# Perceiver kernel: small vectors loaded second, and the second batch's normalisation with statistics instructions and five norms on GpSimd

## The chip, the cores and the metric

The kernel runs on one core of one Trainium2 chip. The core has five engines that this text names as the profile does: PE (TensorE, matmuls, with PEld for its weight loads), DVE (VectorE), ACT (ScalarE), POOL (GpSimd) and SP (SyncE, which here only issues transfers). Each engine takes its instructions in the order in which they stand in its own queue and waits where an instruction needs something that isn't there yet. The metric is the device time of one execution in microseconds, smaller being better.

## What is computed

The input is a set of latents `x` (16 batches of 64 vectors of 128 numbers), a context of 16 batches of 1601 vectors of 128 numbers, and a mask over the context. Two layers follow each other. Each has a cross attention from the latents to the context together with the latents, and then a recurrent scan and a feed-forward part on the latents. The part that matters here is the cross attention of the first layer:

```python
xn = _layernorm(x, ln1_w, ln1_b)            # x: the context, 1601 rows a batch
ln = _layernorm(latents, ln2_w, ln2_b)
q = ln @ Wq                                  # 16 heads of 64
kv = jnp.concatenate([xn, ln], axis=-2) @ Wkv
k, v = jnp.split(kv, 2, axis=-1)
logits = jnp.einsum('bhld,bhsd->bhls', q * scale, k * scale)
out = jnp.einsum('bhls,bhsd->bhld', softmax(logits), v)
return out.reshape(B, L, INNER) @ Wo
```

`_layernorm` subtracts the mean of each row, multiplies by the reciprocal square root of variance plus 1e-5, and applies a weight and a bias.

## The kernel before

**Folding.** The kernel never forms keys and values. It multiplies the query weights with the key weights once (`fold_qk`, in four groups of four heads, L320; the result is the tile `wqk`), so that a score is a product of a folded query (`q`, L429, kept as `qT`) with the normalised context itself. In the same way `fold_vo` (tile `wvo`) merges value and output weights, and the weighted mean (`av`, L669) is taken over the normalised context.

**The context of a batch.** 1600 of its 1601 rows are held as 13 tiles of 128 columns (the last with 64 rows, filled up with the 64 latents of the batch); the remaining row is treated apart. Two forms are needed: `kv`, rows on partitions, and `kvT`, its transpose. Batch 0 is prepared by `first_context` (L467), which takes mean and variance of each tile with a pair of VectorE statistics instructions (L483, L484), raises variance plus EPS to the power −½ on POOL (L487), and has the norms of the 13 tiles done by DVE (tiles 0 to 3), ACT (4 to 7, L519) and POOL (8 to 12, L492). Every other batch of layer 0 goes through `context` (L549): two reductions on DVE give the means (L558), 13 squares with accumulated sums on ACT give the variances (L564), DVE scales them (L568), POOL computes the power (L117, inside the helper `rsqrt`) and the offset (L570), and ACT applies 13 norms (L573). Then the tiles are written to DRAM for layer 1 (`xh`, L576), transposed by PE in groups of four (`kt`, L581), copied to `kvT` by ACT (L582), and multiplied by the norm's weight, in `kvT` on ACT (L590) and in `kv` on POOL (L543, in `with_latents`).

**The main loop.** A group is half the heads of one batch; there are 64 groups, each with 13 steps. In step `n` of `run`, `scores` makes one 128 x 512 block of scores on PE (`s`, L607, in one of three PSUM buffers), ACT copies it out (`st`, L614), and DVE keeps the running maximum (`R`, L621). After the 13 steps the maximum is turned and spread over partitions (`tm`, `mb`), DVE subtracts it from two blocks at a time (L656), ACT takes the exponential (L657), and PE multiplies the result with `kv` (`av`, L669), `LAG` = 21 steps after the scores.

**Order of the work.** The preparation functions are generators. `run` resumes each of them as the steps go by: a list `prep` holds for each the step from which it is resumed, and a `yield` of a number ends its portion for this step, while a `yield` of a tuple (`HOP` and its kin) makes it pause for that many steps. Between the portions, `behind` and `in_order` fix on each engine which instruction may stand behind which. At the very beginning `setup` issues the first transfers and resumes the first generators by an explicit list (L226). The transfers of the start go through two queues: on ACT the first pair of query and key weights (`raw_pair`, L305) and then the 12 small vectors as rows (`vrow`, L202); on SP the first latents `X` (L199), the context of batch 0 in four pieces (`rkv`, L455 and L458) with the other weight pairs between and behind them, the row apart (`xe`), the vectors spread over partitions (`vec`), batch 1 (`kv`, L460) and more latents. PE transposes `vrow` to columns (`vcol`, L221), ACT copies them out (L223) and DVE makes the negative (`nvcol`, L224).

Of the kernel before, what the change touches and what calls it, by code (L numbers as in the profile page):

```python
# [32 lines left out]
F32 = mybir.dt.float32  # L33
# [3 lines left out]
AF = mybir.ActivationFunctionType  # L37
ALU = mybir.AluOpType
# [4 lines left out]
P = 128  # L43
NB, L, D = 16, 64, 128
# [20 lines left out]
HOP1, HOP, HOP3, HOP4 = (1,), (2,), (3,), (4,)  # L65
# [3 lines left out]
EPS, REPS = 1e-5, 1e-6  # L69
# [8 lines left out]
class Kernel:  # L78
# [112 lines left out]
    def setup(self):  # L191
        nc, a = self.nc, self.a
        self.ident = self.cst([P, P], "ident")
        make_identity(nc, self.ident)
        self.neghalf = self.cst([P, 16], "neghalf")
        nc.gpsimd.memset(self.neghalf, -0.5)
        self.X = self.cst([P, C, D], "X")
        xs = a["x"].rearrange("(c p) d -> p c d", p=P)
        nc.sync.dma_start(out=self.X[:, :CG], in_=xs[:, :CG])  # L199
        self.raw0 = [self.raw_pair(0, "WqT", "WkT", 0, nc.scalar)]  # L200
        rows = self.at.tile([12, D], F32, tag="vrow", name="vrow")
        nc.scalar.dma_start(out=rows, in_=a["vec128"].rearrange("(n d) -> n d", d=D))  # L202
        self.context_load(0, 0)
        self.raw0 += [self.raw_pair(0, "WqT", "WkT", g, nc.sync) for g in range(2, H // 4)]
        self.xe = self.cst([NB, D], "xe")
        nc.sync.dma_start(out=self.xe, in_=a["ctx"][:, SK, :])

        self.vec = self.cst([P, 14, D], "vec")
        nc.sync.dma_start(out=self.vec[:, :12].rearrange("p n d -> p (n d)"), in_=a["vec128"].partition_broadcast(P))
        self.context_load(0, 1)  # L210
        nc.sync.dma_start(out=self.X[:, CG:], in_=xs[:, CG:])
        self.xh = [self.dram.tile([P, G + 1, D], F32, tag=f"xh{b}", name=f"xh{b}") for b in range(NB)]
        self.xhT = [self.dram.tile([P, SK], F32, tag=f"xhT{b}", name=f"xhT{b}") for b in range(NB)]


        self.xed = [self.dram.tile([NB, D + 1], F32, tag=f"xed{lay}", name=f"xed{lay}") for lay in range(2)]
        latents, fold, queries, context = self.latents(0, 0), self.fold_qk(0), self.queries(0, 0), self.first_context()
        next(latents)

        t = self.tp("vcol")  # L220
        nc.tensor.transpose(t[:, :12], rows, self.ident[:12, :12])  # L221
        self.vcol, self.nvcol = self.cst([P, 12], "vcol"), self.cst([P, 12], "nvcol")
        nc.scalar.copy(self.vcol, t[:, :12])  # L223
        nc.vector.tensor_scalar_mul(self.nvcol, t[:, :12], -1.0)  # L224

        for g in (context, fold, fold, latents, latents, context, context, queries, queries, context, queries):  # L226
            next(g)
        self.in_order()
        return (0, context), (1, fold), (5, queries), (8, latents)

# [236 lines left out]
    def first_context(self):  # L467


        nc = self.nc  # L470
        kv, kvT = self.kv_of[0, 0]
        w1 = self.vecs_of(0)[0]
        n = G + 1
        mv = self.sm([P, n, 2], "fmv", bufs=1)
        rstd, off = (self.sm([P, n], f"c{x}") for x in ("rstd", "off"))
        rows = lambda k: P if k < G else REM
        first = lambda k: self.raw_kv[k // 8][:rows(k), k % 8, :]

        def stats(lo, hi):
            for k in range(lo, hi):  # L480
                bs = self.sm([P, 6], "fbs")
                p = rows(k)
                nc.vector.bn_stats(bs[:p], first(k))  # L483
                nc.vector.bn_aggr(mv[:p, k, :], bs[:p])  # L484
            p = rows(lo)
            nc.vector.tensor_scalar_add(rstd[:p, lo:hi], mv[:p, lo:hi, 1], EPS)
            nc.gpsimd.tensor_tensor(rstd[:p, lo:hi], rstd[:p, lo:hi], self.neghalf[:p, lo:hi], ALU.pow)  # L487

        def norm(eng, lo, hi):
            for k in range(lo, hi):  # L490
                p = rows(k)
                x = eng.tensor_scalar(kv[:p, k, :D], first(k), mv[:p, k, 0:1], rstd[:p, k:k + 1], ALU.subtract, ALU.mult)  # L492
            if eng is nc.gpsimd:
                self.place["Pool"].append(x.ins)

        def turned(lo, hi):
            m, w = (P, (hi - lo) * P) if hi < n else (REM, REM)
            t = self.tp(f"kt0_{lo}")
            for k in range(lo, hi):
                nc.tensor.transpose(t[:, (k - lo) * P:(k - lo) * P + m], kv[:m, k, :D], self.ident[:m, :m])  # L500
            nc.scalar.activation(kvT[:, lo * P:lo * P + w], t[:, :w], AF.Copy, scale=self.vcol[:, w1:w1 + 1])
            raw = self.at.tile([P, 2, NQ], F32, tag="st2", name=f"xt{lo}", bufs=11)[:, 0, :w]
            nc.vector.tensor_copy(raw, t[:, :w])
            nc.sync.dma_start(out=self.xhT[0][:, lo * P:lo * P + w], in_=raw)

        stats(0, 4)
        yield 0.0
        norm(nc.vector, 0, 4)
        yield 0.0
        stats(4, 8)  # L510
        nc.gpsimd.tensor_tensor(off[:, 4:8], mv[:, 4:8, 0], rstd[:, 4:8], ALU.mult)
        nc.gpsimd.tensor_scalar(off[:, 4:8], off[:, 4:8], -1.0, None, ALU.mult)
        yield 0.0
        turned(0, 4)
        yield 0.0
        stats(8, 12)
        yield 0.0
        for k in range(4, 8):
            nc.scalar.activation(kv[:, k, :D], first(k), AF.Identity, scale=rstd[:, k:k + 1], bias=off[:, k:k + 1])  # L519
            if k % 2:  # L520
                yield 0.0
        norm(nc.gpsimd, 8, 12)
        turned(4, 8)
        yield 0.0
        stats(12, n)
        norm(nc.gpsimd, 12, n)
        yield HOP
        turned(8, 12)
        yield HOP
        turned(12, n)  # L530
        yield 0.0
        nc.sync.dma_start(out=self.xh[0], in_=kv[:, :, :D])
        self.with_latents(0, 0)
        yield 0.0
# [14 lines left out]
    def context(self, lay, b):  # L549

        nc = self.nc
        w1, b1 = self.vecs_of(lay)[:2]
        kv, kvT = self.kv_of[lay, b]
        n = G + 1
        if lay == 0:
            nmean, rstd, v, off = (self.sm([P, n], f"c{x}") for x in ("mean", "rstd", "var", "off"))
            for lo, hi in ((0, 7), (7, n)):
                nc.vector.tensor_reduce(nmean[:, lo:hi], kv[:, lo:hi, :D], AX.X, ALU.add)  # L558
                yield 1.0
            nc.vector.tensor_scalar_mul(nmean, nmean, -1.0 / D)  # L560
            yield 0.2
            for k in range(n):
                scr = self.at.tile([P, D], F32, tag="cscr", name=f"scr{b}_{k}", bufs=1)
                nc.scalar.activation(scr, kv[:, k, :D], AF.Square, bias=nmean[:, k:k + 1], accum_out=v[:, k:k + 1])  # L564
                if k % 5 == 4:
                    yield 0.0
            yield HOP1
            nc.vector.tensor_scalar(v, v, 1.0 / D, 1e-5, ALU.mult, ALU.add)  # L568
            self.rsqrt(rstd, v, n)
            nc.gpsimd.tensor_tensor(off, nmean, rstd, ALU.mult)  # L570
            yield HOP4
            for k in range(n):
                nc.scalar.activation(kv[:, k, :D], kv[:, k, :D], AF.Identity, scale=rstd[:, k:k + 1], bias=off[:, k:k + 1])  # L573
                if k % 5 == 4:
                    yield 0.0
            nc.sync.dma_start(out=self.xh[b], in_=kv[:, :, :D])  # L576
            yield HOP
            for g in range(G // 4):
                t = self.tp(f"kt{b}_{g}")
                for k in range(4):  # L580
                    nc.tensor.transpose(t[:, k * P:(k + 1) * P], kv[:, g * 4 + k, :D], self.ident)  # L581
                nc.scalar.copy(kvT[:, g * 512:(g + 1) * 512], t)  # L582
                yield 0.5
            t = self.tp(f"kt{b}_r")
            nc.tensor.transpose(t[:, :REM], kv[:REM, G, :D], self.ident[:REM, :REM])
            nc.scalar.copy(kvT[:, P * G:SK], t[:, :REM])
            nc.sync.dma_start(out=self.xhT[b], in_=kvT[:, :SK])
            yield HOP3
# [672 lines left out]
    def run(self, out):  # L1261
# [19 lines left out]
        for lay in range(2):  # L1281
# [13 lines left out]
                    prep.append((start(lay, 2 * c) - 16, 1, self.queries(lay, c)))  # L1295
            for b in range(NB):
                if lay or b:
                    prep.append((max(start(lay, b) - (28 if lay == 0 else 12), 4), 2 if lay == 0 else 1, self.context(lay, b)))
                prep.append((start(lay, b) - 2 if lay or b else 12, 1, self.apart_scores(lay, b)))
        prep.sort(key=lambda x: x[0])  # L1300
        live = []
# [190 lines left out]
```

## Time and profile before

| | us |
|---|---|
| median of 3 runs | 2035.77 |
| lowest and highest of them | 2031.73, 2039.77 |
| the profiled execution: device time | 2033.91 |
| the profiled execution: span from first to last instruction | 2032.2 |
| mean granted clock of PE over the span | 0.989 |

The profile is of one execution. Its page gives busy time by engine; an engine's timeline lists its instructions in order of start (start, duration, engine, line, operation, output<-inputs and shapes, and in brackets the idle time ahead of the instruction with what ended it). A table by stretches gives the busy time of each engine in each window of time, in the order PE, PEld, DVE, ACT, POOL, with the number of instructions in brackets, followed by the clock that was granted to PE (1.00 is full), the share of time in which the DMA engines were busy, and the GB/s they moved; asked of one engine, it gives that engine's column alone.

### The profile page before, as it was taken

What the parts mean: (1) busy time and instruction counts of PE and PEld (TensorE: products, weight loads), DVE (VectorE), ACT (ScalarE), POOL (GpSimd) and SP (SyncE); (2) the same over time, 40 slices, a digit from 0 to 9 for tenths busy, and PEclk for the clock granted to TensorE, in tenths of its full rate; (3) what the DMA queues carried; (4) which work ended last, traced back from release to release, by engine and by line L of the source; (5) the groups of instructions that cost most, each with busy time, mean ns of one, the idle gap of its engine ahead of it and who ended that gap; (6) DMA issues with size and microseconds to landing.
All of it is one profiled execution on the core that took longest, in us unless ns stands there. A gap on an engine that the chain in (4) does not pass through costs nothing. (4 is left out here: it accounts for less than half of the span.)

```text
span 2032.2 us, 32648 instructions
## 1 busy us (share of the span) xinstructions
PE 1960.1 (96%) x12005; PEld 1485.8 (73%) x12005; DVE 1556.6 (77%) x2898; ACT 1403.1 (69%) x2667; POOL 515.8 (25%) x576
## 2 busy tenths in 40 slices
PE   8999999999999999999999999999999999999994
PEld 5677777676777767778777787777778777787783
DVE  5887667987878887675988777898686878778774
ACT  5887878887768887566767557776566656675651
POOL 4112122643114452121543203442111121101000
PEclk9999999999999999999999999999999999999996
DMA  5211112322022221221221102211120111101000
GB/s 157 68 53 48 52 52 73 86 63 60 28 86 84 67 71 50 64 76 45 67 80 50 38 22 73 74 57 51 43 58 13 57 36 50 43 1 36 23 1 21
DMA packets 141804, 110.53 MB, mean 54 GB/s; under 512 B 11458, under 2 KB 127950, under 8 KB 141646
## 3 DMA queue, kind: packets, MB, share of 16 engines
q1 hardware_dynamic: 141078, 108.19, 18.2%
q8 instruction: 95, 1.56, 0.3%
q14 instruction: 63, 0.52, 0.1%
q10 hardware_dynamic: 568, 0.27, 0.0%
HBM read 79.97 MB, written 27.41 MB: 53 GB/s over the span
## 5 line engine op out<-in xcount | busy, mean ns | idle before, releaser
L669 PEld LDWEIGHTS av<-kv,st 128*128 128x128 f32 x6656 | 850.5, 192 | 314.8 <-issue 286.5
L669 PE MATMUL av<-kv,st 128*128 128x129 f32 x6656 | 867.8, 276 | 8.3 <-ACT st L657 3.9
L607 PE MATMUL s<-qT,kvT 128*128 128x512 f32 x1664 | 851.0, 601 | 15.7 <-DVE R L621 12.4
L656 DVE TENSOR_TENSOR st<-st,mb 128x1024 f32<-128x1024 f32 (+1 forms) x448 | 501.0, 1131 | 1.7 <-PE mb L648 1.5
L657 ACT ACTIVATE st<-st 128x1024 f32<-128x1024 f32 (+1 forms) x448 | 444.5, 996 | 65.0 <-DVE st L656 61.8
L612 ACT ACTIVATE st<-s,mcol 128x512 f32<-128x512 f32 x416 | 283.8, 685 | 224.6 <-PE s L607 179.5
L614 ACT COPY st<-s 128x512 f32<-128x512 f32 x416 | 240.5, 581 | 128.5 <-PE s L607 103.2
L607 PEld LDWEIGHTS s<-qT,kvT 128*128 128x128 f32 x1664 | 258.8, 192 | 85.0 <-DVE R L621 34.6
L619 DVE SCALAR_TENSOR_TENSOR R<-s,mcol,R 128x512 f32<-128x512 f32 x352 | 261.7, 743 | 70.6 <-ACT st L612 69.4
L621 DVE TENSOR_TENSOR R<-s,R 128x512 f32<-128x512 f32 x352 | 240.7, 684 | 85.8 <-ACT st L614 84.1
L543 POOL TENSOR_TENSOR kv<-kv,vec 128x384 f32<-128x384 f32 (+1 forms) x128 | 134.8, 1073 | 152.1 <-PE kt L581 50.7
L688 POOL TENSOR_TENSOR aq<-aq,rd 128x512 f32<-128x512 f32 x63 | 77.0, 1222 | 357.6 <-DVE rd L685 350.4
L790 POOL TENSOR_TENSOR db<-sc_u,bb 128x512 f32<-128x512 f32 x64 | 86.3, 1352 | 135.7 <-DVE h L801 60.0
L807 POOL TENSOR_TENSOR sc_y<-sc_y,h 128x512 f32<-128x512 f32 x60 | 80.9, 1349 | 101.9 <-DVE h L806 78.8
L573 ACT ACTIVATE kv<-kv,coff,crstd 128x128 f32<-128x128 f32 x195 | 81.5, 488 | 7.5 <-POOL coff L570 7.5
L801 DVE TENSOR_TENSOR_SCAN h<-da,db 128x512 f32<-128x512 f32 x64 | 85.0, 1328 | 0.0
L564 ACT ACTIVATE scr<-kv,cmean 128x128 f32<-128x128 f32 x195 | 78.1, 400 | 7.0 <-DVE cmean L560 3.7
L621 DVE TENSOR_TENSOR R<-s,st 128x512 f32<-128x512 f32 x32 | 22.1, 690 | 73.8 <-ACT st L614 73.8
L678 DVE SCALAR_TENSOR_TENSOR aq<-xeb,ee,av 128x129 f32<-128x129 f32 x256 | 73.8, 340 | 4.5 <-PE av L669 4.5
L117 POOL TENSOR_TENSOR crstd<-cvar,neghalf 128x13 f32<-128x13 f32 x15 | 37.5, 2498 | 140.9 <-DVE cvar L568 140.7
L429 PE MATMUL q<-xnT,wqk 128*128 128x128 f32 x512 | 70.1, 281 | 0.8 <-ACT xnT L164 0.7
L429 PEld LDWEIGHTS q<-xnT,wqk 128*128 128x128 f32 x512 | 64.4, 196 | 7.1 <-issue 3.1
(373 smaller groups left out, 1934.1 us busy)
## 6 DMA issues: line engine op xcount, KB each, us to landing
bb<-bcd SPq DMA_DIRECT2D x64, 256.0 KB, 4.4
xh<-kv SPq DMA_DIRECT2D x16, 832.0 KB, 4.7
kv<-xh SPq DMA_DIRECT2D x16, 832.0 KB, 5.5
kvT<-xhT SPq DMA_DIRECT2D x16, 800.0 KB, 4.6
xhT<-kvT SPq DMA_DIRECT2D x15, 800.0 KB, 3.6
kv<-in_ctx_dram SPq DMA_DIRECT2D x15, 768.0 KB, 5.4
ew<-in_e1T_dram SPq DMA_DIRECT2D x36, 64.0 KB, 1.8
ew<-in_e3T_dram SPq DMA_DIRECT2D x36, 64.0 KB, 1.9
```

Source lines behind the costliest of these rows:

```text
L429: nc.tensor.matmul(t[:, k * P:(k + 1) * P], self.wqk[:, g * 4 + k, :], xnT, start=True, stop=True)
L543: nc.gpsimd.tensor_tensor(kv[:, lo:hi, :D], kv[:, lo:hi, :D], self.row(self.vec[:, w1, :], [P, hi - lo, D]), ALU.mult)
L607: mm = nc.tensor.matmul(s, self.kv_of[lay, b][1][:, i * P:(i + 1) * P], q, start=True, stop=True)
L612: ev = nc.scalar.activation(st, s, AF.Identity, bias=mc)
L614: ev = nc.scalar.copy(st, s)
L619: mx = nc.vector.scalar_tensor_tensor(R, s, mc, last, ALU.add, ALU.max)
L621: mx = nc.vector.tensor_tensor(R, s, last, ALU.max)
L656: nc.vector.tensor_tensor(st, st, self.row(mb, [P, n, NQ]), ALU.subtract)
L657: nc.scalar.activation(st, st, AF.Exp)
L669: nc.tensor.matmul(o, st, self.kv_of[lay, b][0][:, i, :], start=(i == 0 and k % 2 == 0), stop=(i == NT - 1 and k % 2 == 1))
L790: nc.gpsimd.tensor_tensor(db, u, self.row(bb[:, 0, s % 2, :], both), ALU.mult)
L801: nc.vector.tensor_tensor_scan(flat(h), flat(da), flat(db), 0.0, ALU.mult, ALU.add)
```

## The change

Five edits are made.

1. The transfer of the 12 small vectors moves from third on ACT's queue to second on SP's, behind `X`.
2. `nvcol` is made from `vcol` in SBUF, at the end of the setup list, and no longer from PSUM at its head; the setup list resumes the generators in another order, and one `yield` of `first_context` falls away, so that the norms of tiles 0 to 3 and the statistics of tiles 4 to 7 are one portion.
3. For batch 1 of layer 0 alone, `context` takes the statistics with the VectorE pair, two tiles a step; POOL norms tiles 8 to 12 and ACT tiles 0 to 7, two tiles a step. What follows the norms (the write to DRAM, the transposes and the rest) stays.
4. The context of batch 1 is resumed from step 3 on and not from step 4.
5. The tile of means and variances gets two buffers, since batch 0 and batch 1 now both use it.

```diff
         nc.sync.dma_start(out=self.X[:, :CG], in_=xs[:, :CG])
+        rows = self.at.tile([12, D], F32, tag="vrow", name="vrow")
+        nc.sync.dma_start(out=rows, in_=a["vec128"].rearrange("(n d) -> n d", d=D))
         self.raw0 = [self.raw_pair(0, "WqT", "WkT", 0, nc.scalar)]
-        rows = self.at.tile([12, D], F32, tag="vrow", name="vrow")
-        nc.scalar.dma_start(out=rows, in_=a["vec128"].rearrange("(n d) -> n d", d=D))
         self.context_load(0, 0)
...
         nc.scalar.copy(self.vcol, t[:, :12])
-        nc.vector.tensor_scalar_mul(self.nvcol, t[:, :12], -1.0)
-
-        for g in (context, fold, fold, latents, latents, context, context, queries, queries, context, queries):
+
+        for g in (context, fold, latents, latents, context, fold, context, queries, queries, queries):
             next(g)
+        nc.vector.tensor_scalar_mul(self.nvcol, self.vcol, -1.0)
...
-        mv = self.sm([P, n, 2], "fmv", bufs=1)
+        mv = self.sm([P, n, 2], "fmv", bufs=2)
...
         norm(nc.vector, 0, 4)
-        yield 0.0
         stats(4, 8)
...
-        if lay == 0:
+        if (lay, b) == (0, 1):
+
+            mv = self.sm([P, n, 2], "fmv", bufs=2)
+            rstd, off = (self.sm([P, n], f"c{x}") for x in ("rstd", "off"))
+            for k in range(n):
+                bs = self.sm([P, 6], "fbs")
+                nc.vector.bn_stats(bs, kv[:, k, :D])
+                nc.vector.bn_aggr(mv[:, k, :], bs)
+                if k % 2:
+                    yield 1.0
+            nc.vector.tensor_scalar_add(rstd, mv[:, :, 1], EPS)
+            self.rsqrt(rstd, rstd, n)
+            nc.gpsimd.tensor_tensor(off, mv[:, :, 0], rstd, ALU.mult)
+            nc.gpsimd.tensor_scalar(off, off, -1.0, None, ALU.mult)
+            for k in range(8, n):
+                nc.gpsimd.tensor_scalar(kv[:, k, :D], kv[:, k, :D], mv[:, k, 0:1], rstd[:, k:k + 1], ALU.subtract, ALU.mult)
+            yield HOP3
+            for k in range(8):
+                nc.scalar.activation(kv[:, k, :D], kv[:, k, :D], AF.Identity, scale=rstd[:, k:k + 1], bias=off[:, k:k + 1])
+                if k % 2:
+                    yield 1.0
+        elif lay == 0:
             nmean, rstd, v, off = (self.sm([P, n], f"c{x}") for x in ("mean", "rstd", "var", "off"))
...
+        if lay == 0:
             nc.sync.dma_start(out=self.xh[b], in_=kv[:, :, :D])
             yield HOP
...
-                    prep.append((max(start(lay, b) - (28 if lay == 0 else 12), 4), 2 if lay == 0 else 1, self.context(lay, b)))
+                    prep.append((max(start(lay, b) - (28 if lay == 0 else 12), 3), 2 if lay == 0 else 1, self.context(lay, b)))
```

## The prediction

> **What bounds the kernel now.** I read the busy shares of the page first, then the same shares by stretch, to see where the busiest engine is not busy.
>
> ```profile
> span 2032.2 us, 32648 instructions
> PE 1960.1 (96%) x12005; PEld 1485.8 (73%) x12005; DVE 1556.6 (77%) x2898; ACT 1403.1 (69%) x2667; POOL 515.8 (25%) x576
> ```
>
> ```profile
> 0.00:60.00 60.00, 47.25 (x219) 31.02 (x220) 35.57 (x95) 35.86 (x91) 21.43 (x45) 0.97 0.55 147
> 60.00:1990.00 1930.00, 1894.96 (x11712) 1441.37 (x11710) 1503.01 (x2752) 1358.69 (x2557) 491.69 (x526) 1.00 0.18 53
> 1990.00:2033.00 43.00, 17.90 (x78) 13.47 (x78) 17.98 (x51) 8.58 (x20) 2.65 (x6) 0.60 0.01 2
> ```
>
> The columns after the width are the busy times of PE, PE's weight loads, DVE, ACT and POOL, then PE's granted clock. From 60 to 1990 us PE is busy 98% of the time, so whatever makes PE reach 60 us earlier ends the kernel earlier by as much, and whatever happens beside PE is free. PE idles 12.75 us in the first 60, and the edits act there: the built order of the changed kernel differs from the old one on every engine only in about the first 100 us of this trace, and is the same, instruction for instruction, behind it.
>
> The timeline shows the idle time in two lumps.
>
> ```profile
> 6.88 0.25 PE L221 MATMUL vcol<-ident,vrow 12*128 12x12 f32 x1 [6.88 <-DMA vrow<-in_vec_dram]
> 7.37 0.17 DVE L224 TENSOR_SCALAR nvcol<-vcol 128x12 f32<-128x12 f32 x1 [3.60 <-ACT vcol L223]
> ...
> 46.35 2.46 POOL L117 TENSOR_TENSOR crstd<-cvar,neghalf 128x13 f32<-128x13 f32 x1 [8.12 <-DVE cvar L568]
> 49.14 2.42 ACT L573 ACTIVATE kv<-kv,coff,crstd 128x128 f32<-128x128 f32 x6 [2.43 <-POOL coff L570]
> 51.56 2.79 ACT L573 ACTIVATE kv<-kv,coff,crstd 128x128 f32<-128x128 f32 x7
> 54.25 0.57 ACT L614 COPY st<-s 128x512 f32<-128x512 f32 x1
> 54.72 1.06 ACT L657 ACTIVATE st<-st 128x1024 f32<-128x1024 f32 x1
> 55.92 1.78 PE L669 MATMUL av<-kv,st 128*128 128x129 f32 x8 [3.11 <-ACT st L657]
> ```
>
> First lump: PE's first instruction waits for the vector rows, the third transfer on ACT's queue, and DVE's first statistics stand behind a copy of their transpose. Second lump: the 13 norms of batch 1 come late (their squares end at 45.86), stand in one block on ACT from 49.14 to 54.35, and hold back the score copies and exponentials behind them. PE starves for 3.11 us and then runs slowly:
>
> ```profile
> 58.00:59.00 1.00, 1.00 (x2) 0.50 0.55 167
> ```
>
> ```profile
> 820.00:830.00 10.00, 10.00 (x66) 1.00 0.11 40
> 830.00:840.00 10.00, 10.00 (x51) 0.72 0.19 54
> ```
>
> The four 1-us stretches from 56 to 60 were granted 0.61, 0.50, 0.50 and 0.68: 0.39+0.50+0.50+0.32 = 1.71 us of full-rate work lost.
>
> **Start of the program.** vrow goes from third on ACT (issued 2.19) to second on SP (1.28). X, first there, lands 2.1 us after its issue; vrow should land near 3.5, so PE's next need, the first weight pair, decides: its second half was issued at 1.53 on ACT and landed 4.2 us later, at 5.73. Fold 0 then starts at 5.85 instead of 7.06: 1.2 earlier. SP's later issues each slip by one issue, some 0.5 us (the X issue took 0.43, the next began 0.49 after it). rkv tiles land 3.6 to 4.6 us after issue; from 1.78, with an almost empty queue, I take 3.7: 5.5. The four statistics with the EPS add took 7.46 to 9.35, 1.9 us; now 5.5 to 7.4, since nvcol no longer stands ahead (it costs 0.17 later, beside PE's work). xn follows (0.60) by 8.0; PE's transpose 0.69, 8.7; fold 1, whose weights landed at 2.54+4.8 = 7.3, now 7.8, runs 8.7 to 10.6 (16 instructions took 3.78, so 1.9). The transpose kt of context 0 moves ahead of the queries, 0.9 at this slow rate; queries take 3.5 as before, to 15.0; the last ACT copy ends at 15.4, and the key evacuation, which used to come after it (16.16 to 16.85), is done by 12.1. First score at 15.5 against 16.90: **−1.4**. Bounds: if the slow rate of the first matmuls (queries 3.51 for 16 instructions, later 1.16 for 8) ends before the queries, they take 2.3 and I get −2.6; if vrow needs 4.65 us as on ACT, it lands at 5.9 and about 1.2 stays. The later X, vec and batch loads are needed only past 14 us. Later in SP's order xed rises and mask and kv_2 drop a few places; their readers come at 25.7, 66 and 67 us.
>
> **Batch 1's statistics.** Removed: on DVE two reductions (1.06+0.93) and two small ones (0.17+0.16), 2.3; on ACT 13 squares with their read-outs (0.40+0.19 each), 7.7, and five norms of 0.40, 2.0. Added: on DVE 13 pairs of 0.26+0.17, 5.6, net +3.3, starting about 4 us earlier in the order; on POOL five norms at 0.80 (row L492) and one 0.24, 4.2. The power of 13 columns, 2.46, remains. DVE is busy 14.82 us between 20 and 45, so 3.3 fit into 10.2 idle; POOL is busy 0.00 between 40 and 45. So both are hidden; without that cover DVE's 3.3 would delay the running maxima, and with three score buffers PE itself.
>
> Chain after the change: the last context-0 norm, the write of xh (5.1 us to landing) and four multiplications on POOL (3.88) end at 36.2; the EPS add stands behind the eighth maximum and a ge copy, 36.5; power to 39.05, offsets with one norm between them 40.45; ACT's norms begin at 40.5, with the copies of scores 11 and 12 queued behind the first of them, and PE behind those copies. Two norms and a copy: score 11 is out at 41.9. PE needs that buffer at 42.4. I see 0.5 us of slack and no stall. From there ACT interleaves one to three norms with each copy and has caught up near 46.5. At mb (48.07 before, 46.8 now) the first exponential waits only for the first subtraction, not for seven norms: **−3.1** for the gap.
>
> The rate penalty goes with it. [...] The row shows 0.50 right behind that gap, so I take **−1.7** more. The 830:840 row, slow with PE never idle, warns that gaps are not the only trigger.
>
> What is late next: in the changed order, subtractions and exponentials 4 to 6 of the first group come later, among the reductions of batch 2, where DVE has 33.93 and ACT 33.26 busy of 40 us (60 to 100). Two subtractions (1.13 each) move into this crowd. Nearest row: PE idles 0.67 us there now. I put **+0.7** (0 to +3).
>
> [...] By the row, POOL norms took 795 to 817 ns while DVE's maxima beside them stayed at 0.69: the last POOL norm ends near 43.7. [...] the transpose that reads it is due near 51. Nothing in the sum either way.
>
> Sum: −1.4 −3.1 −1.7 +0.7 = **−5.5 us**. On the profiled execution (2033.91 us, span 2032.2) that gives 2028.4. The median shown is 1.9 above that execution; all four times average 2035.3, so I forecast **2029.8**. About 0.5%, 10 us, is what a measurement of this kernel can tell from no change; −5.5 is inside.
>
> **Rivals**, on the same 2035.3.
> - *The stall moves to the crowd after 60 us.* For it: ACT and DVE are in order and over 83% busy there. Against: the total of ACT work falls by 9.7. Cost +3 instead of +0.7: 2032.1.
> - *The rate helps more.* Full rate one step earlier (−1.2 more), no crowding (−0.7), and the slow stretch at 834 us, 6.8 us at half, falls away (−3.4; the trace shows no reason for its place): 2024.5. Against: nothing in the change touches that place.
> - *Slower: ACT blocked behind POOL.* The norms stand ahead of the copies of scores 11 and 12. If POOL's power comes later than planned, each us beyond the 0.5 stalls PE one for one. At about 6 us late the gain is used up; at 8 us, −5.5+7.5+1.7 (slow rate after so long a gap) = +3.7: 2039.0. For it: POOL waited 10.5 us for one xh write further on. Against: this write is issued earlier than before.
> - *It does less than it says*: vrow no earlier, or the squares were no cause: 2034.
>
> **How the numbers follow.** Forecast 0.50, moved stall 0.20, rate 0.17, blocked ACT 0.07, no effect 0.06. The three runs of before span 8 us, so a median wanders by 2 to 3. Range 2022.5 to 2037: the forecast's own bounds (start −2.6 to −1.2, rate −1.7 to 0, crowd 0 to +3: sums of −7.4 to −1.3, 2027.9 to 2034.0) with that wander, most of the rate case, and the milder half of the blocked one. Faster by over 0.5% means below 2025.1: most of the rate case and the lower tail of the forecast, 0.20. Slower by over 0.5% needs the blocked case and bad luck: 0.04. The rest, 0.76, is no change.
>
> **What would show it.** Right: vcol before 5 us, first score near 15.5, norms on ACT between score copies from about 40.5, no PE gap over 1 us between 50 and 56, no slow rate there, and PE work of 60 us done 5 to 6 us earlier. Wrong: a PE wait on ACT copies near 42, or on exponentials past 60; a first matmul still near 7; or a gain that is gone by 100 us.

## The result, and the profile after

| kernel | median of the runs, us | ratio to before (95%) | profiled execution, us | span, us | granted clock |
|---|---|---|---|---|---|
| before (11 runs) | 2035.55 | 1 | 2033.91 | 2032.2 | 0.989 |
| changed (11 runs) | 2028.82 | 0.9969 (0.9960 to 0.9978) | 2027.75 | 2026.0 | 0.991 |
| changed, measured again (11 runs) | 2028.85 | 0.9960 (0.9947 to 0.9973) | 2031.14 | 2029.4 | 0.988 |

The ratio of 0.9969 is −6.3 us on 2035.55, between −4.5 and −8.1. The second ratio is to 50 runs of the kernel before on another chip (median 2037.66): −8.2 us. The forecast was 2029.8 us, −5.5 on the profiled execution, and no change that a measurement can tell from none. From one profiled execution to the other the difference is −6.2.

The page of the changed kernel begins with the span, then the busy time of each engine:

```profile
span 2026.0 us, 32647 instructions
PE 1957.4 (97%) x12005; PEld 1485.0 (73%) x12005; DVE 1558.6 (77%) x2921; ACT 1395.5 (69%) x2636; POOL 518.8 (26%) x582
```

PE has the same 12005 matmuls. ACT has 31 instructions fewer and DVE 23 more, which is the change itself. The busy times by stretch (PE, its weight loads, DVE, ACT, POOL, then PE's clock) show where the time came from:

```profile
0.00:60.00 60.00, 53.21 (x257) 35.18 (x258) 39.54 (x129) 35.29 (x72) 29.11 (x54) 1.00 0.61 166
60.00:1990.00 1930.00, 1887.40 (x11679) 1437.11 (x11679) 1504.48 (x2751) 1352.64 (x2548) 487.07 (x522) 1.00 0.18 52
1990.00:2033.00 43.00, 16.75 (x73) 12.71 (x73) 14.59 (x42) 7.55 (x17) 2.66 (x6) 0.64 0.01 2
```

In the first 60 us PE works 53.21 us instead of 47.25, starts 257 matmuls instead of 219, and the clock column reads 1.00 instead of 0.97. Behind 60 us it idles 42.6 us of 1930 instead of 35.0, partly because the sparse end of the kernel now begins before 1990. The timeline of the first 55 us, all engines, shows the steps:

```profile
3.98 0.25 PE L221 MATMUL vcol<-ident,vrow 12*128 12x12 f32 x1 [3.98 <-DMA vrow<-in_vec_dram]
6.00 2.04 PE L320 MATMUL WqT<-rawWqT 64*128 64x128 f32 x8 [1.76 <-DMA rawWqT<-in_L0WkT_dram]
6.04 0.29 DVE L483 BATCH_NORM_STATS2 fbs<-rkv 128x6 f32<-128x128 f32 x1 [1.97 <-DMA rkv<-in_ctx_dram]
15.89 1.12 PE L628 MATMUL s<-qT,kvT 128*128 128x512 f32 x2 [0.46 <-ACT qT L434]
35.62 2.46 POOL L117 TENSOR_TENSOR crstd<-crstd,neghalf 128x13 f32<-128x13 f32 x1 [0.32 <-DVE crstd L564]
39.38 3.15 POOL L569 TENSOR_SCALAR kv<-kv,fmv,crstd 128x128 f32<-128x128 f32 x4
39.44 0.88 ACT L572 ACTIVATE kv<-kv,coff,crstd 128x128 f32<-128x128 f32 x2 [2.28 <-POOL coff L567]
40.23 0.56 ACT L635 COPY st<-s 128x512 f32<-128x512 f32 x1
46.29 0.62 PE L669 MATMUL mb<-ident,m 128*128 128x128 f32 x4
48.77 1.07 ACT L678 ACTIVATE st<-st 128x1024 f32<-128x1024 f32 x1
```

The norms stand between the score copies from 39.44, the first exponential starts at 48.77 instead of 54.72, and no row of PE between 46 and 56 has a wait in brackets.

A landmark makes the later readings short. PE's second `mb` product (the transposition that spreads the maxima of group 2) is the first one behind the old gap. It starts at 79.99 us before and at 72.22 after: 7.77 earlier. Comparing the k-th score product of both traces, the lead is 1.0 at the first, 1.8 at the first `mb`, 7.8 at 72 us, 6.4 at 131, 5.6 at 362, 4.8 at 771, 7.9 at 852 and 6.2 at the end.

### The profile page after: what moved, and what is told of

Read it like the earlier page. It is cut to its first block, busy times and chain, and to the rows that moved or that the text cites. A ratio compares the mean times of both kernels' runs of the same rounds, so it can differ in the third digit from the quotient of the medians.

```text
span 2026.0 us, 32647 instructions
## 1 busy us (share of the span) xinstructions
PE 1957.4 (97%) x12005; PEld 1485.0 (73%) x12005; DVE 1558.6 (77%) x2921; ACT 1395.5 (69%) x2636; POOL 518.8 (26%) x582
## 5 line engine op out<-in xcount | busy, mean ns | idle before, releaser
L593 ACT ACTIVATE kv<-kv,coff,crstd 128x128 f32<-128x128 f32 x182 | 76.4, 488 | 5.1 <-POOL coff L590 5.1
L584 ACT ACTIVATE scr<-kv,cmean 128x128 f32<-128x128 f32 x182 | 72.8, 400 | 6.9 <-DVE cmean L580 3.7
```

## The experiments

All ratios are to the kernel before, run beside the experiment on the same chip, and differences in us are the ratio times the median of those runs, if nothing else is said; kernels run once have no ratio. "Second mb" is the landmark above.

| kernel | median, us | ratio (95%) | second mb, us |
|---|---|---|---|
| start of the program alone | 2034.4 | 0.9992 (0.9979 to 1.0006) | 77.97 |
| batch 1's recipe alone | 2031.2 | 0.9977 (0.9966 to 0.9988) | 74.77 |
| all 13 norms of batch 1 on ACT | 2027.81, one run | – | 74.94 |
| old statistics, five norms on GpSimd | 2031.16 | 0.9980 (0.9967 to 0.9992) | 76.99 |
| old statistics, all norms on ACT | 2036.12 | 0.9989 (0.9980 to 0.9999) | 77.99 |
| filler matmuls in the old gap | 2036.56 | 1.0007 (0.9994 to 1.0019) | 78.96 |
| left-over set-up work later | 2030.74 | 0.9974 (0.9966 to 0.9983) | 71.91 |
| recipe for all batches | 2041.27 | 1.0029 (1.0009 to 1.0049) | 72.25 |
| the same, longer distance | 2040.72 | 1.0013 (1.0001 to 1.0026) | 73.29 |
| the same, later norms all on ACT | 2028.71 | 0.9953 (0.9936 to 0.9971) | 73.03 |

**The two halves apart.** First the start alone (batch 1 keeps its old branch), then batch 1's recipe alone (the order of the first transfers and steps is the old one).

```diff
-        if (lay, b) == (0, 1):
+        if (lay, b) == (0, NB):
...
-  ... - (28 if lay == 0 else 12), 3), 2 if lay == 0 else 1, self.context(lay, b)))
+  ... - (28 if lay == 0 else 12), 4), 2 if lay == 0 else 1, self.context(lay, b)))
```

> The edits to the start alone; batch 1 keeps its reductions, squares and 13 norms on ACT. Landmarks: the first score on PE (16.90 us before, 15.89 after) and the second spreading of a maximum, mb of the second group (79.99 before, 72.22 after). Theory (the start is worth 1.0 us, the norms' block the rest): first score at 15.9, PE gap of about 3 us and the slow clock still there between 50 and 60, second mb near 79.0, total about 1 us faster. Rival (the order of the setup list also loosens what follows): second mb below 77, total 3 us or more faster.

> Batch 1's new statistics and norms alone; the start as before. Theory: first score at 16.9, no PE gap over 1 us between 45 and 60, second mb near 73.2 (6.8 below before), total about 5.5 us faster. Rival (the gains need each other, because the norms are ready in time only if the start is early): second mb above 75.

Measured: −1.6 us (0.9992, which holds 1) and −4.7 us (0.9977); their sum, −6.3, is within the intervals what the whole change gives. In the kernel with the start alone the first score comes at 15.43 (−1.47), but PE meets two waits:

```profile
40.58 1.27 PE L320 MATMUL WvT<-rawWvT 64*128 64x128 f32 x8 [1.30 <-DMA rawWvT<-in_L0Wo_dram]
53.61 1.13 PE L628 MATMUL s<-qT,kvT 128*128 128x512 f32 x2 [3.00 <-DVE R L642]
```

The first is the transfer of a later weight, the second the old gap, as long as before. In the old order the same products start at 41.53 with no wait in brackets; with an earlier start it waits, and the clock is half from 41.4 to 44.8. At the first `mb` (48.70) this execution is 0.6 behind that of before; at the second it is 2.0 ahead, but mainly because the half clock that before has behind the gap is missing here. So what the earlier start is worth by itself stays open (−4.3 to +1.2 us by the interval). With the recipe alone there is no gap, and the landmark is 5.2 earlier: 74.77, between the 73.2 of the theory and the 75 of its rival.

**Which part of the recipe does it.** Three variants of the changed kernel: all 13 norms on ACT; the old reductions and squares with five norms on GpSimd (run once, then 20 times); the old statistics with all norms on ACT, but two a step.

```diff
-            for k in range(8, n):
-                nc.gpsimd.tensor_scalar(kv[:, k, :D], kv[:, k, :D], mv[:, k, 0:1], rstd[:, k:k + 1], ALU.subtract, ALU.mult)
             yield HOP3
-            for k in range(8):
+            for k in range(n):
```

```diff
-                bs = self.sm([P, 6], "fbs")
-                nc.vector.bn_stats(bs, kv[:, k, :D])
-                nc.vector.bn_aggr(mv[:, k, :], bs)
...
+                nc.scalar.activation(scr, kv[:, k, :D], AF.Square, bias=nmean[:, k:k + 1], accum_out=v[:, k:k + 1])
```

> The changed kernel with all 13 norms of batch 1 on ACT, two a step, and none on POOL. Theory (it is the early statistics and the small portions that count; ACT has room between 45 and 48): second mb within 0.7 us of 72.2. Rival (POOL's five norms are what frees ACT): PE waits for ACT copies or for the late norms, second mb at 74 or later.

> The changed kernel with the old statistics of batch 1 (two reductions on DVE, 13 squares on ACT) but the new norms (five on POOL, eight on ACT, two a step). Theory (the norms were late because the squares stood among the copies on ACT until 45.9): the norms come some 3 to 5 us later than in the changed kernel, PE waits 1 to 3 us, second mb at 73.5 to 75.5. Rival (only the block of 13 mattered): second mb within 0.7 us of 72.2.

> The earlier kernel again (the change with the old reductions and squares for batch 1's statistics, five norms still on GpSimd), because its one look had a half-clock stretch of 13.65 us at 36.95 that hid the rest. Theory A[...]: it does not come back or comes elsewhere, second mb near 73 us (after: 72.22), and the time near 2029 to 2031. Theory B (my prediction's chain: squares on ACT delay the norms, so PE starves before the first av): second mb 75 us or later with an idle gap of 1 us or more between 44 and 56, at full clock. Theory C (this order of instructions itself lowers the clock): half clock again between 35 and 52, second mb near 79.8, time near 2035.

> The change without its statistics instructions and without norms on GpSimd: old reductions and 13 squares, all 13 norms on ACT, but norms two a step and the start two... one step earlier, and the new start of the program. Theory (the gap went because the norms no longer stand in one block ahead of the copies and exponentials; the statistics only shorten the chain): no gap of over 1 us at 50 to 56, second mb at 73 to 76, ratio 0.9975 to 0.9985. Rival (the chain's length decides: old squares end 4 us later, so the norms collide with the subtractions and exponentials of the first group): a gap of 1.5 us or more at 52 to 62, second mb at 77 or later, ratio 0.9985 to 1.0000. In both, PE's wait for the transfer of rawWvT near 40.6 (1.30 and 1.11 us in the two kernels with new start and old statistics) may come back, with half clock behind it.

With 13 norms on ACT the exponentials come later and a wait appears right behind the first values, from PE's timeline:

```profile
60.02 1.13 PE L626 MATMUL s<-qT,kvT 128*128 128x512 f32 x2 [1.61 <-DVE R L640]
```

The landmark is 2.7 later than in the change, as the rival had it, but at 105 us only 1.1 of that is left (lead 5.6 against 6.7), and the two executions end level (2027.81 and 2027.75 us). With one run of this variant, what the five norms on GpSimd are worth in the total is not shown.

The old statistics with five norms on GpSimd gave half clock in both profiles: 13.65 us of it in the first (2035.96 us in all) and 6.83 us in the second. Without the 3.4 us that this costs, the landmark of the second would be 73.6, as theory A expects; that slow stretches came back in the same place speaks for theory C. Measured over 20 runs, the variant keeps −4.1 us. Its PE waits for the weight again and is then slow while it is busy (PE's timeline, and the 2-us stretches):

```profile
40.64 1.71 PE L320 MATMUL WvT<-rawWvT 64*128 64x128 f32 x8 [1.11 <-DMA rawWvT<-in_L0Wo_dram]
```

```profile
42.00:44.00 2.00, 2.00 (x8) 1.19 (x8) 0.76 (x2) 1.65 (x4) 1.85 (x5) 0.50 0.75 161
44.00:46.00 2.00, 2.00 (x3) 0.57 (x2) 0.00 (x0) 1.29 (x3) 0.55 (x2) 0.50 0.00 0
```

With norms two a step as the only thing left of the recipe, the gap at 50 to 56 is gone too (PE's longest wait there is 0.3), as the theory has it. But landmark (77.99) and ratio (0.9989, −2.2 us) are those of the rival: the variant pays a slow stretch near 38 us, a wait of 0.82 at 63, and smaller ones. In the slow stretch a pair of score products takes twice the 1.02 us of the pair at 45.42:

```profile
38.03 2.08 PE L629 MATMUL s<-qT,kvT 128*128 128x512 f32 x2
```

So the interleaving removes the visible gap, but most of the time saved needs the rest of the recipe. How much of that is the statistics and how much GpSimd's norms stays open: the intervals of the two variants overlap (0.9980 to 0.9999, 0.9967 to 0.9992).

**The price of the old gap's slow clock.** The kernel before, with 15 transposes of normalised tiles in the gap:

```diff
+            if g == 0:
+                fill = self.kv_of[0, 1][0]
+                for k in range(8, 13):
+                    for r in range(3):
+                        nc.tensor.transpose(grp["av"][:, 0, 384:512], fill[:, k, :D], self.ident)
```

> The kernel before, with 15 extra TensorE transposes (128x128, of normalised tiles 8 to 12 of batch 1, into unused columns of the av accumulator) put into the gap ahead of the first av matmul. They depend on data that is there by about 54.5 us, so they fill some 1 us of the 3.11 us gap and add nothing in time if they end before the exponential that PE waits for (54.72 + 1.06 = 55.8). Theory (the idle gap causes the half clock of 56 to 60 us): no half clock behind the gap, second mb some 1.7 us earlier than before (79.99 to about 78.3). [...] If the transposes come late they cost up to 1.0 us themselves. Total: 2032 to 2036 us.

PE resumes 0.65 later than before (a lag that it has at the first `mb` already), but at full clock (stretches, last columns PE's clock, DMA share and GB/s):

```profile
56.57 1.13 PE L674 MATMUL av<-kv,st 128*128 128x129 f32 x8 [0.97 <-ACT st L657]
```

```profile
56.00:60.00 4.00, 3.43 (x20) 2.41 (x20) 4.00 (x6) 4.00 (x8) 0.25 (x1) 1.00 0.68 213
```

Against the trace of before, the lag of 0.64 turns into a lead of 1.03: 1.67 us, which is the 1.71 of the prediction. The runs can neither show nor exclude so little: 1.0007 is −1.2 to +3.9 us by its interval, and the lead in the trace is 1.0. The kernel with the start alone had 3.00 us of the same gap with full clock behind it. So the term is real in the two executions compared here, and not a saving in each execution; what decides between half and full clock behind such a gap is not shown.

**What is given back behind the gap.** In the changed kernel, PE's first wait after the gap, and ACT's in front of it:

```profile
85.34 2.92 PE L690 MATMUL av<-kv,st 128*128 128x129 f32 x24 [1.19 <-ACT kv L593]
```

```profile
80.51 1.26 ACT L593 ACTIVATE kv<-kv,coff,crstd 128x128 f32<-128x128 f32 x3 [1.67 <-POOL coff L590]
```

ACT waits 1.67 for the offsets of batch 2, which still has the old recipe, and its copies stand behind. To see whether the set-up work in that stretch is the crowd, it was moved 13 steps later:

```diff
-        between.append((LAG, 0.8, self.setup_rest()))
+        between.append((LAG + 13, 0.8, self.setup_rest()))
```

> The changed kernel with the left-over set-up work (setup_rest) started 13 steps later, so that its instructions leave the crowded stretch of 60 to 100 us. Theory (the 1.3 us given back between 72 and 130 us, predicted 0.7, is crowding of DVE and ACT by that work): PE waits there shrink, and progress at 130 us is 1 us or more ahead of the change: -7.4 against before in place of -6.4. Rival (batch 2's block of norms on ACT, in the line of copies and reductions, causes it): no change at 130 us, or the set-up work crowds a later stretch and costs the same there. Total 2027.5 to 2029.

At 105 us the lead is 8.3 instead of 6.7, so the set-up work has a part in the crowd there. Then a like wait comes later, and the lead is 6.9 at 131 us and 5.0 at 159, less than the change's 6.4:

```profile
140.64 1.12 PE L628 MATMUL s<-qT,kvT 128*128 128x512 f32 x2 [1.29 <-DVE R L642]
```

```profile
137.57 0.88 ACT L593 ACTIVATE kv<-kv,coff,crstd 128x128 f32<-128x128 f32 x2 [1.64 <-POOL coff L590]
```

The second half of the rival holds: the work crowds a later stretch and costs no less there, and the total is that of the change within the intervals (0.9974 against 0.9969 and 0.9960).

**The recipe everywhere.** `if lay == 0` in place of `if (lay, b) == (0, 1)`; then with each context begun 4 steps earlier and 7 steps instead of 3 before ACT's norms; then the same with all later norms on ACT.

```diff
-            yield HOP3
+            yield HOP3 if b == 1 else (7,)
...
-  (28 if lay == 0 else 12), 3)
+  (32 if lay == 0 else 12), 3)
```

```diff
-            for k in range(8, n):
+            for k in range(8 if b == 1 else n, n):
                 nc.gpsimd.tensor_scalar(...)
...
-            for k in range(8):
+            for k in range(8 if b == 1 else n):
```

> The changed kernel with the new recipe (statistics instructions, five norms on GpSimd, norms two a step) for all batches of the first layer, not only for batch 1. Per batch it takes 9.7 us from ACT and adds 3.3 to DVE. Theory (past 60 us PE waits on ACT's block of norms of each batch): PE's waits on ACT between 80 and 820 us shrink, and the kernel is 2 to 5 us faster than the change (2024 to 2027). Rival (DVE, 77% busy and the releaser of most score waits, becomes the late one, and GpSimd's power and offsets then hold ACT): PE waits on DVE grow and the kernel is level with or slower than the change by 1 to 6 us (2029 to 2035).

> The new recipe for all batches of layer 0, as before, but from batch 2 on begun 4 steps earlier and with 7 steps instead of 3 between GpSimd's offsets and the first norm on ACT. Theory (with the recipe everywhere, ACT stood idle 5.09 us at 363 waiting for GpSimd's offsets, whose power was queued behind GpSimd's product of the scan, and the score copy behind that norm held PE for 3.72 us): ACT's waits for coff past 60 us fall from 13.3 us to under 3, PE's waits on R from 17.8 to 12 or less, and the kernel is level with the change or up to 4 us faster (2025 to 2030). Rival (VectorE's added 3.3 us a batch is the cost, not the wait on GpSimd): PE's waits on R stay at 15 us or more though ACT no longer waits for coff, 2032 or more.

> As the kernel with the longer distance, but from batch 2 on all 13 norms stay on ACT (GpSimd does the power and the offsets only). Theory (GpSimd's five norms, 4 us a batch in front of the scan's products, delay the scan and so VectorE): a little faster than with norms on GpSimd, by 0 to 2 us. Rival (ACT is the tighter engine near the scan): slower by 1 to 3 us. Level with the change within 3 us in both.

The first is slower than before by 5.9 us; my theory had it faster. It shows, near 363 us, the prediction's slower rival in full (timeline, POOL, ACT and PE):

```profile
358.41 1.27 POOL L828 TENSOR_TENSOR sc_y<-sc_y,h 128x512 f32<-128x512 f32 x1 [4.37 <-DVE crstd L564]
359.64 2.46 POOL L117 TENSOR_TENSOR crstd<-crstd,neghalf 128x13 f32<-128x13 f32 x1
363.46 0.49 ACT L572 ACTIVATE kv<-kv,coff,crstd 128x128 f32<-128x128 f32 x1 [5.09 <-POOL coff L567]
365.20 3.89 PE L628 MATMUL s<-qT,kvT 128*128 128x512 f32 x4 [3.72 <-DVE R L642]
```

POOL's power stands behind a product of the scan, which had to wait for its operand from DVE (the row names the EPS add of 358.18, which DVE issued just behind that operand, 357.60 to 358.26). ACT's first norm waits 5.09 us for the power and the offsets, the score copy behind it waits too, and PE starves. The clock is half from 364 to 371 (the same form of four score products takes 1.98 us at 396.67), and reads 0.94 over 340 to 400.

With the longer distance ACT no longer waits for the offsets (13.3 us in four waits past 60 us before that edit, none after), and PE's waits for the running maxima fall from 17.8 to 13.0 us. The kernel is still slower than before (2040.72), which neither theory nor rival explains. Something else has come, near 608 us (timeline, POOL, DVE and PE):

```profile
603.06 3.15 POOL L569 TENSOR_SCALAR kv<-kv,fmv,crstd 128x128 f32<-128x128 f32 x4
606.29 0.47 POOL L136 TENSOR_SCALAR var<-mv 128x2 f32<-128x2 f32 x2
608.27 0.48 DVE L143 TENSOR_SCALAR sc_xn<-X,mv,rstd 128x128 f32<-128x128 f32 x1 [7.47 <-POOL rstd L117]
610.56 1.08 PE L669 MATMUL mb<-ident,m 128*128 128x128 f32 x4 [5.25 <-DVE tm L660]
```

Now the batch's power and its five norms on POOL (7 us from 599.3) stand ahead of the small power that the scan's normalisation needs; DVE waits 7.47 us for it with the maxima queued behind, and PE 5.25. Without those five norms, everything else equal, the kernel runs in 2028.71 instead of 2040.72 us. My theory for this run had 0 to 2 us for it, and the measurement says 12. Between the two traces about 5 of these 12 us arise from 600 to 660 us, around this stall, and about 4 more from 850 to 950, and that the norms cause the second part is not shown. A norm on POOL costs little by itself (0.79 us each in the row of four) and much by what is queued behind it. The 3.3 us that the statistics add to DVE in each batch cost nothing that could be seen. This last kernel has the best ratio, 0.9953, but beside the change on the same chip (0.9960, medians 2028.71 and 2028.85) it is level with it.

**The change again.**

> The changed kernel once more, beside the variants of this call, and for a second profile. Theory (the gain of 60 us is real work saved[...]): second mb again near 72.2, no idle gap over 1 us between 20 and 60, a ratio to before of 0.996 to 0.998. Rival (the measured gain was partly the absence of the half-clock stretch at 834 us in that one profile): a half-clock stretch near 834 turns up in this profile; the ratio is then still 0.997, since it is of many runs.

The ratio is 0.9960, at the edge of what was expected. The landmark came at 74.37 and not near 72.2, though behind the first 10 us no wait of PE over 0.6 us stands ahead of it: 3.41 us at half clock, which cost 1.7 of the 2.15 us between them, fell just before, from 63.1 to 66.5, while PE was busy throughout:

```profile
63.00:67.00 4.00, 4.00 (x17) 2.97 (x16) 4.00 (x9) 1.09 (x3) 0.00 (x0) 0.57 0.28 82
```

No slow stretch turned up near 834 us.

## Why the prediction was right, step by step

The total was right within its range, and it is right for the mechanism it names: the gap ahead of the first values closes because batch 1's norms come earlier and between the copies. Inside the sum the terms are off in both directions.

- **Start, −1.4.** Measured −1.0 in the first profile, −1.5 in the kernel with the start alone; `vcol` at 3.98, fold 0 at 6.00 for 5.85. In the first profile `rkv` was later than my sum, at about 6.0 and not 5.5. Over all traces the term is right: the first score comes at 16.90 to 17.41 with the old start (three traces, mean 17.23) and at 15.03 to 16.30 with the new one (eleven, mean 15.82). Another 0.8 of lead until the first `mb` (46.29, predicted 46.8) comes from PE's small waits between 24 and 42 us, 0.9 us before and 0.1 after, which I had not counted.
- **Chain of the norms.** Power 1 us earlier than my sum (35.62 to 38.1), norms on ACT at 39.44 for 40.5, score 11 copied by 40.8 with no stall. The slack was larger than my 0.5.
- **Gap, −3.1.** Under-sized. From the first to the second `mb` the lead grows by 6.0: 3.1 of idle time, 1.7 of clock, and 1.1 that was hidden as work. In the trace of before a block of transposes reads norms that ACT is just finishing:

```profile
49.69 1.48 PE L581 MATMUL kt<-ident,kv 128*128 128x128 f32 x4 [0.16 <-ACT kv L573]
```

  In the changed kernel the same four take 0.60:

```profile
47.61 0.60 PE L602 MATMUL kt<-ident,kv 128*128 128x128 f32 x4
```

  I take the 0.88 us between them as waits that the row does not put in brackets.
- **Clock, −1.7.** I had taken this from the row with half clock behind a gap of 3.11 us. The filler shows that the row was right for that trace, and the kernel with the start alone shows 3.00 us of gap with full clock behind it (1.00 from 54 to 60). Gaps of nearly one length went either way, and what decides is not shown. The sum took the one outcome it had seen as certain.
- **Crowd, +0.7.** Measured 1.35 by 131 us. The place was right. PE's longest wait there (1.19) is for batch 2's own norms on ACT and not for the later exponentials of the first group; moving the set-up work only moved the loss. Another 1.7 is given back up to 771 us, at waits on the running maxima, which the prediction did not have.
- **Behind that** the profile of before lost 3.4 us in its slow stretch at 834, and that of after has none, which moves the lead from 4.8 to 7.9. I had this only in a rival, and saw no reason for its place; the traces show none. Without it the two profiles would differ by 3 us; the ratios give 6.3 and 8.2. So the sum met the two profiles partly by luck: an under-sized gap, an under-sized return and a stretch of the clock cancel.
- **Rivals.** "The stall moves" holds for the size of the return, not the total. "ACT blocked behind POOL" did not come with batch 1, and came with the same recipe in later batches, as the kernel with the recipe everywhere shows. A norm does take longer on POOL. The norms of batch 0, one tensor as input, have the same operation on both engines in the trace of before, and POOL takes 2.8 times as long for four:

```profile
10.51 1.11 DVE L492 TENSOR_SCALAR kv<-rkv,fmv,crstd 128x128 f32<-128x128 f32 x4 [0.66 <-POOL crstd L487]
21.14 3.16 POOL L492 TENSOR_SCALAR kv<-rkv,fmv,crstd 128x128 f32<-128x128 f32 x4
```

  In the changed kernel four of batch 1's take 3.15 us, as in that row, and DVE's maxima beside them stay at 0.69, with one operand in PSUM. So the norms are slow there, but POOL had the time; what speaks against GpSimd here is its queue.

## What to carry to other kernels

Work that is cheap for an engine with idle time is judged by what stands behind it in that engine's queue: one recipe gave −4.7 us in a place where POOL had nothing else to do, and with five norms per batch on POOL a kernel 12 us slower than with them on ACT. When a stall is removed, follow the progress of the bounding engine against the old trace to the end, since part of the gain can come back at the next meeting of the same queues (here 1.35 us by 131 us). A gain of 0.3% is a matter of many runs: two profiles can agree with a sum whose terms are wrong.

## What the hardware did that was not expected

PE's clock halves for some us at a time: in the kernel before from 56.2 us for 3.41 and from 834.5 for 6.83, in the changed one's second profile from 63.1 for 3.41, and in the two profiles with the old statistics and five norms on GpSimd for 13.65 and 6.83. The first profile of the changed kernel has no such stretch ahead of its last 80 us. An idle gap as the only cause does not fit: PE is busy for all 4.00 us from 830 to 834 in the kernel before, and for all 3.00 us from 60 to 63 in the changed one's second profile. Nor does the length of a gap tell by itself, as far as two gaps show it: behind 3.11 us in the kernel before the clock is 0.57 from 56 to 60, behind 3.00 us with the start alone it is 1.00 from 54 to 60.

Just ahead of the stretch at 834 us, products on 64 and 32 rows (the first number of a weight's shape) stand in PE's timeline:

```profile
831.47 1.13 PE L320 MATMUL WqT<-rawWkT,rawWqT 64*128 64x128 f32 x8
832.53 2.05 PE L910 MATMUL mo<-w_fWoT,mo_oT 32*128 32x128 f32 x16
```

In the first profile of the changed kernel the same products start at 826.78 and 827.84, take the same 1.13 and 2.05 us, and the clock reads 1.00 from 815 to 840. No run here changed the rows alone, so what brings a slow stretch about is not shown.

The clock goes with most of the scatter. Of the 11 runs of the changed kernel the four at 0.991 took 2025.07 to 2027.75 us, the four at 0.987 and 0.988 took 2029.6 to 2030.82: between their means 3.6 us for 0.0033 of clock, about 1.1 us for 0.001. The mean clock of before was 0.9885 in 31 runs on one chip and 0.9879 in 50 on another, that of the change 0.9894 and 0.9889 in 11 runs each, 0.001 more. So about 1 us of the difference between the kernels goes with the clock; how much of that the order of instructions brings about is open.
